# A graph attention layer on one core: two tiles of sources picked on the chip from the first step on, from parts of x made in the prologue

## The chip, the cores and the metric

The kernel runs on one core of a Trainium2 chip. The metric is the device time of one execution in microseconds (us): before the change the median of 10 runs is 3075.61 us (3069.55 to 3079.59). Lower is better.

A core has five engines with queues of their own: PE (TensorE, matmuls; the profile shows its weight loads apart as PEld), DVE (VectorE), ACT (ScalarE), POOL (GpSimd, which here issues the indirect DMAs) and SP (SyncE, which issues plain DMAs). Each works through its instructions in order and waits on semaphores for the others.

## The reference

One layer of attention over the edges of a graph with 6250 nodes and 206250 edges, 64 channels in 4 heads of 16, then a residual and a layer norm. The edges are sorted by destination.

```
Qh, Kh, Vh = x @ Wq.T + bq, x @ Wk.T + bk, x @ Wv.T + bv      # per node, 4 heads of 16
Ee = edge_attr @ We.T + be                                    # per edge
score = (Kh[src] * Qh[dst] * (1 / sqrt(16)) * Ee).sum(-1)
score = exp(clip(score, -5, 5))
msg = Vh[src] * score[..., None]
wV = segment_sum(msg, dst, num_segments=6250)
out = layernorm(x + wV)
```

## The kernel before

**Tiles, groups, steps.** A tile is 128 edges, one on each partition; there are 1612. Eight tiles are a group (202 groups), and a step is two groups, save for the last eight steps, which are one group each. So steps 0 to 96 have 16 tiles and steps 97 to 104 have 8 (the last one 4). `STEPS`, `NS` = 105, `groups_of`, `tiles_in` say this in the code.

**Prologue.** From the transposed x in SBUF (`xT_sb`, one column for each node) PE makes k and v of all nodes, which go to a table in HBM (`kv_tab`), and q in three bf16 parts, which go to another. POOL meanwhile gathers the rows of x for the sources of the first four groups (`XS`, L230). At the end of the prologue a loop over these four groups in halves of four tiles (from L370) turns them on PE (L375), copies the turned x to SBUF on ACT (L378, `xe`), multiplies it with the weights of k and v (L380, L382) and copies the result into the kv buffers (L384). So steps 0 and 1 need no gather. POOL gathers groups 4 to 7 (steps 2 and 3) from `kv_tab` (L402), one indirect DMA for a tile. Then a value is read that says whether a window of destinations is too wide; it isn't, and the main part follows.

**The main part** runs over the steps. For a step s, in short:

- `spread`, `onehot_rows`, `queries` (L555, L572, L577, L595): each edge's q comes from a window of rows of the q table (`fetch_queries`), by a matmul with a one-hot of its destination. They are made for step s+1 within step s.
- `edges` (L388, L391): the edge values.
- `products`, `scores`, `message` (L602, L603, L609 to L612, L619): DVE multiplies k, q and the edge values, reduces them to scores, and multiplies v with them. The multiplication with v, L619, is the last reader of the step's kv buffer. There are five such buffers (`KVB`), and `gather(s + 4)` on POOL waits for L619 of step s-1.
- `minus` (L622, L630, L632): the message is split in three bf16 parts. `sums` (L638): a matmul with a one-hot of destinations adds the message by destination, one step later; `add` (L652) adds it to the accumulator.
- `close`, `spreads`, `roots`, `norm`: finished blocks of 128 nodes are normalised and stored.

**Picks.** For the last two tiles of a step, k and v aren't gathered. Step s prepares this for step s+2, when `picks_in(s)` holds: s from 4 to `LAST` = 94. `sources` (ACT, L466) and `sources_turned` (PE, L471) spread the sources of the tile over the partitions; `hots` (DVE, L481) makes one-hots of all 50 blocks of nodes in two instructions for each tile; `picks` (PE, L491) multiplies them with the table `parts`: x of all nodes in three bf16 parts, 50 blocks of 128 nodes by 192 columns. That is 100 matmuls a step, in four quarters of 25. `picked`, `picked_turned` and `picked_kv` (L498, L505, L507, L513 to L516) add the three parts, turn the picked rows of x and make k and v of them. In the steps with picks 14 of 16 tiles are gathered. In every sixth step from 12 on one more tile is fetched by rows through SP (`fetch_rows`, L544), so that 13 are gathered.

**The table `parts`** lies in the pool `accp` of the main part and is filled in steps 0 to 3: a memset (L427), then for blocks of 8 (`TB`) a load of x by SP into `raw` (L448), two copies by ACT (L450, L451) and in `table_parts_rest` two subtractions by DVE (L456, L458) with a copy by ACT between them (L457).

The order in all queues is the program's order, written out by hand (the loop `for s in range(NS)` at the end of the main part); nothing is moved by a scheduler.

Of the kernel before, what the change touches and what calls it, by code (L numbers as in the profile page):

```python
# [37 lines left out]
CB = 10  # L38
KVB = 5
XG = 4  # L40
TB = 8
M0 = 4
PAD = N
SPARE = N + 1
TABLES = 4
# [15 lines left out]

LAST = NS - 8 - 3


def picks_in(s):
    return M0 <= s <= LAST

# [33 lines left out]
def tile_gnn(ctx: ExitStack, tc: tile.TileContext, x, xT, wT, bias, beT, weT, eT, src, dst, dst_rows,  # L103
# [50 lines left out]
    be_p = consts.tile([3, G, C], BF16, name="be_p")  # L154
    wkv = consts.tile([P, 2, 2 * C], F32, name="wkv")
    bkv_p = consts.tile([3, G // 2, 2 * C], BF16, name="bkv_p")
    minus_b = consts.tile([P, P], BF16, name="minus_b")

    acc = consts.tile([P, RING, 4, C], F32, name="acc")
# [24 lines left out]
    with tc.tile_pool(name="nodes", bufs=1) as nodes, \  # L184
# [182 lines left out]
            fetch_queries(g)  # L367


        for g in range(XG):  # L370
            for h in range(2):
                tp = npsum.tile([P, 2, P], F32, name="tp", bufs=2)
                for u in range(2):
                    j = 4 * h + 2 * u
                    nc.tensor.transpose(tp[:, u, :],  # L375
                                        XS[g][:, j:j + 2, :].rearrange("p j c -> p (j c)"), ident)
                xe = nodes.tile([P, 2, P], F32, name="xe", bufs=2)
                nc.scalar.activation(xe, tp, AF.Copy)  # L378
                pv = npsum.tile([P, 4, 2 * C], F32, name="pv", bufs=2)
                nc.tensor.matmul(pv, ones_b, bkv_p, start=True, stop=False, skip_group_check=True)  # L380
                for u in range(2):
                    nc.tensor.matmul(pv[:, 2 * u:2 * u + 2, :], xe[:, u, :], wkv, start=False,  # L382
                                     stop=u == 1, skip_group_check=True)
                nc.scalar.activation(kv_of(g)[:, 4 * h:4 * h + 4, :], pv, AF.Copy)  # L384

    def edge_values(pe, et, n):

# [6 lines left out]
    def keys(t0):  # L394

        n = min(KEYS, T - t0)
        nc.vector.tensor_scalar(key_i[:, :n], dst_i[:, t0:t0 + n], P - 1, None, op0=OP.bitwise_and)
        nc.vector.tensor_copy(key[:, t0:t0 + n], key_i[:, :n, None].to_broadcast([P, n, 2]))

    def gather_kv(g, j):  # L400
        t = g * G + j
        nc.gpsimd.indirect_dma_start(  # L402
            out=kv_of(g)[:, j, :], out_offset=None, in_=kv_tab[:, :],
            in_offset=bass.IndirectOffsetOnAxis(ap=src_i[:, t:t + 1], axis=0))

    for g in range(XG, 2 * KVB - 2):
        for j in range(G):
            gather_kv(g, j)

    rv = nc.values_load(n_wide[0:1, 0:1], min_val=0, max_val=NR2 * 4)  # L410

    with tc.If(rv == 0) as branch:

        with tc.tile_pool(name="work", bufs=2) as work, \
# [8 lines left out]
            pa = small[:, 4 * C:7 * C].rearrange("p (i c) -> p i c", i=3)  # L423
            nc.tensor.transpose(col, row_b[:, 0:1].to_broadcast([P, P]), ident_b)

            parts = accp.tile([P, NB, 3, C], BF16, name="parts")
            nc.vector.memset(parts, 0.0)  # L427
            NX = N // NB
            x_v = x.rearrange("(p b) c -> p b c", p=NX)
            n_picks = LAST - M0 + 1  # L430
            src_f = accp.tile([P, n_picks, 2], F32, name="src_f")
            t0 = (M0 + 3) * 2 * G - 2
            for i in range(2):
                nc.vector.tensor_copy(src_f[:, :, i],
                                      src_i[:, t0 + i:t0 + i + 2 * G * (n_picks - 1) + 1:2 * G])
            pick = fixed.tile([P, 4 * P], F32, name="pick")
            rows3 = pick[:, :6 * C].rearrange("p (k i c) -> p k i c", k=2, i=3)
            HOT, FAR, X = {}, {}, {}
# [2 lines left out]

                return ap.rearrange("p (a b) -> p a b", b=2)

            def table_parts(b):

                n = min(TB, NB - b)
                raw = work.tile([P, TB, C], F32, name="raw", bufs=1)
                nc.sync.dma_start(raw[:NX, :n], x_v[:, b:b + n, :])  # L448
                rest = pick[:NX, :n * C].rearrange("p (b c) -> p b c", b=n)
                nc.scalar.activation(rest, raw[:NX, :n], AF.Copy)  # L450
                nc.scalar.activation(parts[:NX, b:b + n, 0], raw[:NX, :n], AF.Copy)  # L451
                return rest

            def table_parts_rest(b, rest):
                n = min(TB, NB - b)
                nc.vector.tensor_sub(rest, rest, parts[:NX, b:b + n, 0])  # L456
                nc.scalar.activation(parts[:NX, b:b + n, 1], rest, AF.Copy)  # L457
                nc.vector.tensor_sub(parts[:NX, b:b + n, 2], rest, parts[:NX, b:b + n, 1])  # L458

            def sources(s, i):  # L460

                if picks_in(s):
                    FAR[s, i] = work.tile([P, P], BF16, name="far")
                    nc.scalar.activation(FAR[s, i], row50, AF.Identity,  # L466
                                         bias=src_f[:, s - M0, i:i + 1], scale=-1.0)
# [42 lines left out]
            def picked_kv(s):  # L510
                if picks_in(s):
                    xe, kv = X.pop(s)
                    nc.tensor.matmul(kv, ones_b, bkv_p[:, :2], start=True, stop=False,  # L513
                                     skip_group_check=True)
                    nc.tensor.matmul(kv, xe, wkv, start=False, stop=True, skip_group_check=True)
                    nc.scalar.activation(kvs[(s + 2) % KVB][:, 2 * G - 2:, :], kv, AF.Copy)  # L516

            def gather(s):
                for g in groups_of(s):
                    for j in range(tiles_of(g)):  # L520
                        if is_rowed(s) and (g - STEPS[s][0]) * G + j == COLUMN:
# [58 lines left out]
            def onehot_edges(s):  # L580

                n, t0 = tiles_in(s), STEPS[s][0] * G
                OH[s] = work.tile([P, 2 * G, P], BF16, name="of")
                shape = [P, n, P // 2, 2]
                nc.vector.tensor_tensor(OH[s].rearrange("p t (a c) -> p t a c", c=2)[:, :n],  # L585
                                        pairs(col)[:, None].to_broadcast(shape),
                                        key[:, t0:t0 + n, None, :].to_broadcast(shape),
                                        op=OP.is_equal)
# [109 lines left out]
                                               op0=OP.mult, op1=OP.add)  # L698

            closed, scaled, normed = 0, 0, 0  # L700
            keys(0)
            for k, g in enumerate(groups_of(0)):
                onehot_rows(g, spread(g))
# [1 line left out]
                edges(0, k)  # L705
            queries(0)
            onehot_edges(0)
            for s in range(NS):
                more = s + 1 < NS
                for g in groups_of(s):  # L710
# [58 lines left out]
                if more:  # L769
# [29 lines left out]
    with branch.Else():  # L799

        sums = [dram.tile([NR, C], F32, name=f"sums{i}") for i in range(TABLES)]
        with tc.tile_pool(name="gconsts", bufs=1) as gc, \
                tc.tile_pool(name="gloads", bufs=3) as loads, \
                tc.tile_pool(name="ggath", bufs=4) as gath, \
# [28 lines left out]
            def gather(g, j):  # L833
                if j == 0:
                    Q[g] = gath.tile([P, G, C], F32, name="gq")
                t = g * G + j
                if g >= 2 * KVB - 2:
# [125 lines left out]
```

## Time and profile before

| | |
|---|---|
| median of 10 runs | 3075.61 us (3069.55 to 3079.59) |
| the profiled execution | 3076.17 us |
| its span, first to last instruction | 3074.4 us |
| mean granted clock of PE | 0.783 |
| busy: PE, PEld | 1982.7 us (64%), 1556.1 us (51%) |
| busy: DVE, ACT, POOL | 1503.4 us (49%), 917.4 us (30%), 1337.2 us (43%) |
| indirect gathers of kv (L402) | 1383, 1305.1 us on POOL |
| matmuls of the picks (L491) | 9100, 1042.5 us on PE |
| one-hots for the picks (L481) | 364, 651.4 us on DVE |

No engine is busy all the time, so shares of busy time don't tell what bounds the kernel; it has to be read from the length of single steps and what they wait for. In the profile a line such as `L491 PE MATMUL pick<-parts,hot` names the line of the code, the engine, the operation, and the tile written and those read. In a timeline, a line starts with the start and the duration of a run of such instructions; behind it stand, in brackets, the idle time of the engine before it and what ended that. "Issue" means that the profile shows nothing that it waited for; "remote" that the event which ended it can't be matched with an instruction. Times of the timeline are us from the start of the span.

### The profile page before, as it was taken

What the parts mean: (1) busy time and instruction counts of PE and PEld (TensorE: products, weight loads), DVE (VectorE), ACT (ScalarE), POOL (GpSimd) and SP (SyncE); (2) the same over time, 40 slices, a digit from 0 to 9 for tenths busy, and PEclk for the clock granted to TensorE, in tenths of its full rate; (3) what the DMA queues carried; (4) which work ended last, traced back from release to release, by engine and by line L of the source; (5) the groups of instructions that cost most, each with busy time, mean ns of one, the idle gap of its engine ahead of it and who ended that gap; (6) DMA issues with size and microseconds to landing.
All of it is one profiled execution on the core that took longest, in us unless ns stands there. A gap on an engine that the chain in (4) does not pass through costs nothing. (4 is left out here: it accounts for less than half of the span.)

```text
span 3074.4 us, 44286 instructions
## 1 busy us (share of the span) xinstructions
PE 1982.7 (64%) x15751; PEld 1556.1 (51%) x15751; DVE 1503.4 (49%) x1695; ACT 917.4 (30%) x1328; POOL 1337.2 (43%) x1427
## 2 busy tenths in 40 slices
PE   5546666757666666757566666757576666667675
PEld 4324554545455554545454554545454555545553
DVE  3244545545454545545454545545454545455554
ACT  2242232323233223323232322323232332223234
POOL 5454435344443434344444435344444434353332
PEclk9967878878787877778787877778787878777885
DMA  5222212111111212121211212121212112121121
GB/s 150 66 78 59 55 44 59 51 49 52 46 48 51 56 43 56 53 57 45 54 52 46 55 44 57 43 57 44 59 47 55 47 52 56 43 57 43 51 56 32
DMA packets 109970, 166.71 MB, mean 54 GB/s; under 512 B 69196, under 2 KB 71452, under 8 KB 109626
## 3 DMA queue, kind: packets, MB, share of 16 engines
q0 software_dynamic: 45280, 91.78, 11.7%
q1 hardware_dynamic: 64074, 71.01, 8.2%
q8 instruction: 125, 2.05, 0.3%
q10 hardware_dynamic: 384, 1.00, 0.2%
q14 instruction: 107, 0.88, 0.1%
HBM read 156.33 MB, written 7.33 MB: 53 GB/s over the span
## 5 line engine op out<-in xcount | busy, mean ns | idle before, releaser
L402 POOL DMA_INDIRECT kv<-kv_tab,src_i x1383 | 1305.1, 944 | 1680.7 <-DVE pq L619 1243.0
L491 PE MATMUL pick<-parts,hot 128*128 128x192 bf16 x9100 | 1042.5, 275 | 251.7 <-issue 251.2
L491 PEld LDWEIGHTS <-hot 128*128 128x128 bf16 x9100 | 892.0, 110 | 378.4 <-issue 322.8
L481 DVE TENSOR_TENSOR hot<-small,block 128x3200 bf16<-128x3200 bf16 x364 | 651.4, 1818 | 286.8 <-remote 246.1
L595 PE MATMUL pq<-qw,to 126*128 126x64 bf16 x1612 | 166.2, 221 | 682.3 <-issue 613.6
L572 ACT ACTIVATE to<-pb,minus_row 126x1024 bf16<-126x1024 f32 x202 | 222.9, 1103 | 971.7 <-PE pb L555 922.5
L602 DVE TENSOR_TENSOR prod<-kv,pq 128x1024 f32<-128x1024 f32 (+2 forms) x105 | 123.7, 1178 | 784.4 <-PE pq L595 406.0
L595 PEld LDWEIGHTS <-to 126*128 126x128 bf16 x1612 | 109.2, 113 | 755.6 <-issue 752.3
L632 ACT ACTIVATE msg<-pq 128x1024 bf16<-128x1024 f32 (+2 forms) x210 | 207.6, 989 | 751.7 <-remote 512.7
L391 PE MATMUL pe<-we_sb,et 128*128 128x128 f32 x1612 | 246.4, 298 | 0.0
L391 PEld LDWEIGHTS pe<-we_sb,et 128*128 128x128 f32 x1612 | 206.6, 201 | 54.0 <-issue 47.6
L577 ACT ACTIVATE to<-to,one_p 126x1024 bf16<-126x1024 bf16 x202 | 230.4, 1141 | 3.5
L609 DVE TENSOR_REDUCE small<-prod 128x64 f32<-128x1024 f32 (+2 forms) x105 | 124.4, 1185 | 196.0 <-PE small L471 147.7
L638 PEld LDWEIGHTS <-of 128*128 128x128 bf16 x1612 | 156.7, 108 | 49.1 <-issue 39.2
L638 PE MATMUL small<-msg,of 128*128 128x192 bf16 x1612 | 171.5, 265 | 0.5 <-ACT msg L632 0.5
L630 PE MATMUL pq<-msg,minus_b 128*128 128x512 bf16 x404 | 128.1, 396 | 66.0 <-ACT msg L622 54.1
L555 PE MATMUL pb<-key_rows,ident_b 112*128 112x512 bf16 x403 | 152.6, 467 | 7.3 <-ACT to L572 4.1
L622 ACT ACTIVATE msg<-pq 128x1024 bf16<-128x1024 f32 (+2 forms) x105 | 103.8, 989 | 96.0 <-DVE pq L619 96.0
L603 DVE TENSOR_TENSOR prod<-prod,pe 128x1024 f32<-128x1024 f32 (+2 forms) x105 | 123.6, 1177 | 3.6
L619 DVE TENSOR_TENSOR pq<-kv,small 128x1024 f32<-128x1024 f32 (+2 forms) x105 | 123.5, 1176 | 1.3 <-ACT small L612 1.3
L585 DVE TENSOR_TENSOR of<-small,key 128x2048 bf16<-128x2048 bf16 (+2 forms) x105 | 123.2, 1174 | 0.3
L498 DVE TENSOR_REDUCE xp<-pick 128x128 f32<-128x384 f32 x91 | 50.7, 558 | 103.3 <-PE pick L491 103.3
(129 smaller groups left out, 991.4 us busy)
## 6 DMA issues: line engine op xcount, KB each, us to landing
et<-in_eT SPq DMA_DIRECT2D x100, 512.0 KB
rk<-kv_tab SPq DMA_DIRECT2D x1920, 0.5 KB
kv<-kv_tab,src_i POOLq DMA_INDIRECT x1383
qw<-q_tab SPq DMA_DIRECT2D x202, 15.8 KB
kv_tab<-kv_sb SPq DMA_DIRECT2D x5, 640.0 KB
q_tab<-q SPq DMA_DIRECT2D x5, 480.0 KB
acc<-in_x SPq DMA_DIRECT2D x48, 32.0 KB
out<-y SPq DMA_DIRECT2D x48, 32.0 KB
```

The source lines that it names most:

```text
L391: nc.tensor.matmul(pe[:, 2 * u:2 * u + 2, :], et[:, u, :], we_sb, start=False, stop=u == n // 2 - 1, skip_group_check=True)
L402: nc.gpsimd.indirect_dma_start(out=kv_of(g)[:, j, :], out_offset=None, in_=kv_tab[:, :], in_offset=bass.IndirectOffsetOnAxis(ap=src_i[:, t ...
L481: nc.vector.tensor_tensor(HOT[s, i, h].rearrange("p b (a c) -> p b a c", c=2), pairs(from_b[i])[:, None].to_broadcast(shape), block2[:, bl ...
L491: nc.tensor.matmul(rows3[:, i], hot[:, k, :], parts[:, b], start=b == 0, stop=b == NB - 1)
L555: nc.tensor.matmul(pb[:, b:b + 4, :], ident_b[:NR2, g // 2:g // 2 + 1].to_broadcast([NR2, P]), key_rows[:, g % 2, b * P:(b + 4) * P], star ...
L572: nc.scalar.activation(TO[g][:, :n, :], pb[:3 * W, :n, :], AF.Square, bias=minus_row3[:3 * W])
L577: nc.scalar.activation(TO[g][:, :n, :], TO[g][:, :n, :], AF.Relu, bias=one_p[:3 * W], scale=-1.0)
L595: nc.tensor.matmul(PQ[s][:, (g - STEPS[s][0]) * G + j, :], TO[g][:, j, :], QW[g], start=j == 0, stop=j == tiles_of(g) - 1, skip_group_chec ...
L609: nc.vector.tensor_reduce(score, prod[:, :n, :].rearrange("p g (h d) -> p g h d", h=H), axis=AX.X, op=OP.add)
L630: nc.tensor.matmul(msg[:, lo:hi, :], minus_b, M3[s][:, lo:hi, i, :], start=False, stop=True, skip_group_check=True)
L632: nc.scalar.activation(M3[s][:, :n, i + 1, :], msg[:, :n, :], AF.Copy)
L638: nc.tensor.matmul(PA[s], OH[s][:, j, :], M3[s][:, j], start=j == 0, stop=j == n - 1)
```

## The change

- The table `parts` moves from `accp` to the constants and is made in the prologue, within the loop over the first four groups. `x_turned` does the turning of a half, `first_kv` its matmuls and copy; the next half is turned before the present one is multiplied. Between them stand `parts_of_x` for two blocks of four (`TB` is now 4): PE turns columns of `xT_sb` into a PSUM tile (`ps`, four buffers), ACT copies the first part, DVE subtracts it; and behind `first_kv`, `rest_of_x` makes the second and third part. All 50 blocks are made so, in the first seven of eight halves.
- The memset, the loads of `raw` and the copies and subtractions in steps 0 to 3 go away, `table_parts` and `table_parts_rest` with them.
- Picks run from step 0 to `LAST` = 96, instead of 4 to 94. So the picked tiles are those of steps 2 to 98, of which 97 and 98 are of one group (`picked_kv` and `src_f` allow for 8 tiles). `sources`, `sources_turned` and `hots` for step 0 stand before the loop.
- `is_picked` says for a tile whether it is picked; the gathers of such tiles are left out, in the prologue (groups 5 and 7) too.
- The branch for too wide windows, which isn't taken, gathers what is missing and has one buffer less in `ggath`.

```diff
-TB = 8
-M0 = 4
+TB = 4
...
-LAST = NS - 8 - 3
+LAST = NS - 8 - 1
 
 def picks_in(s):
-    return M0 <= s <= LAST
+    return 0 <= s <= LAST
+
+def is_picked(g, j):
+    s = max(s for s in range(NS) if STEPS[s][0] <= g)
+    return picks_in(s - 2) and g == groups_of(s)[-1] and j >= G - 2
...
+    parts = consts.tile([P, NB, 3, C], BF16, name="parts")
...
-        for g in range(XG):
-            for h in range(2):
...
+        def x_turned(g, h):
+            tp = npsum.tile([P, 2, P], F32, name="tp", bufs=2)
+            for u in range(2):
+                j = 4 * h + 2 * u
+                nc.tensor.transpose(tp[:, u, :], XS[g][:, j:j + 2, :].rearrange("p j c -> p (j c)"),
+                                    ident)
+            xe = nodes.tile([P, 2, P], F32, name="xe", bufs=2)
+            nc.scalar.activation(xe, tp, AF.Copy)
+            return xe
+
+        def first_kv(g, h, xe):
+            pv = npsum.tile([P, 4, 2 * C], F32, name="pv", bufs=2)
+            nc.tensor.matmul(pv, ones_b, bkv_p, start=True, stop=False, skip_group_check=True)
+            for u in range(2):
+                nc.tensor.matmul(pv[:, 2 * u:2 * u + 2, :], xe[:, u, :], wkv, start=False,
+                                 stop=u == 1, skip_group_check=True)
+            nc.scalar.activation(kv_of(g)[:, 4 * h:4 * h + 4, :], pv, AF.Copy)
+
+        halves = []
+
+        def parts_of_x(b):
+            n = min(TB, NB - b)
+            px = npsum.tile([P, 2, 2 * C], F32, name="ps").rearrange("p i (j c) -> p (i j) c", j=2)
+            px = px[:, :n]
+            for u in range(n):
+                nc.tensor.transpose(px[:, u, :], xT_sb[:C, (b + u) * P:(b + u + 1) * P],
+                                    ident[:C, :C])
+            nc.scalar.activation(parts[:, b:b + n, 0], px, AF.Copy)
+            nc.vector.tensor_sub(px, px, parts[:, b:b + n, 0])
+            halves.append((px, b, n))
+
+        def rest_of_x():
+            px, b, n = halves.pop(0)
+            nc.scalar.activation(parts[:, b:b + n, 1], px, AF.Copy)
+            nc.vector.tensor_sub(parts[:, b:b + n, 2], px, parts[:, b:b + n, 1])
+
+        order = [(g, h) for g in range(XG) for h in range(2)]
+        blocks = list(range(0, NB, TB))
+        xe = x_turned(*order[0])
+        for i, gh in enumerate(order):
+            following = x_turned(*order[i + 1]) if i + 1 < len(order) else None
+            for b in blocks[2 * i:2 * i + 2]:
+                parts_of_x(b)
+            first_kv(*gh, xe)
+            xe = following
+            while halves:
+                rest_of_x()
...
     for g in range(XG, 2 * KVB - 2):
         for j in range(G):
-            gather_kv(g, j)
+            if not is_picked(g, j):
+                gather_kv(g, j)
...
-            parts = accp.tile([P, NB, 3, C], BF16, name="parts")
-            nc.vector.memset(parts, 0.0)
...
+            src_f = accp.tile([P, LAST + 1, 2], F32, name="src_f")
+            full = NS - 8 - 2
             for i in range(2):
...
+            for s in range(full, LAST + 1):
+                t0 = STEPS[s + 2][0] * G + G - 2
+                nc.vector.tensor_copy(src_f[:, s], src_i[:, t0:t0 + 2])
...
-                    nc.scalar.activation(kvs[(s + 2) % KVB][:, 2 * G - 2:, :], kv, AF.Copy)
+                    n = tiles_in(s + 2)
+                    nc.scalar.activation(kvs[(s + 2) % KVB][:, n - 2:n, :], kv, AF.Copy)
...
-                        if not picks_in(s - 2) or g == STEPS[s][0] or j < G - 2:
+                        if not is_picked(g, j):
                             gather_kv(g, j)
...
+            sources(0, 0)
+            sources_turned(0, 0)
             keys(0)
...
             onehot_edges(0)
+            sources(0, 1)
+            sources(1, 0)
+            for h in range(2):
+                hots(0, 0, h)
             for s in range(NS):
...
-                making = [b for b in range(s * 2 * TB, (s + 1) * 2 * TB, TB) if b < NB]
-                if making:
-                    rest = table_parts(making[0])
...
-                for i, b in enumerate(making):
-                    if i:
-                        rest = table_parts(b)
-                    table_parts_rest(b, rest)
```

More of the change, by code (lines that the diff above doesn't have):

```diff
@@ L367, in tile_gnn @@
             fetch_queries(g)
-        for g in range(XG):
-            for h in range(2):
[L372 to L384, printed above, removed]
+        def x_turned(g, h):
[7 more added lines that the diff above has]
+            return xe
@@ L424, in tile_gnn @@
             nc.tensor.transpose(col, row_b[:, 0:1].to_broadcast([P, P]), ident_b)
-            parts = accp.tile([P, NB, 3, C], BF16, name="parts")
-            nc.vector.memset(parts, 0.0)
[L428 to L432, printed above, removed]
-            for i in range(2):
-                nc.vector.tensor_copy(src_f[:, :, i],
-                                      src_i[:, t0 + i:t0 + i + 2 * G * (n_picks - 1) + 1:2 * G])
+            src_f = accp.tile([P, LAST + 1, 2], F32, name="src_f")
+            full = NS - 8 - 2
+            for i in range(2):
+                t0 = 3 * 2 * G - 2 + i
+                nc.vector.tensor_copy(src_f[:, :full, i],
+                                      src_i[:, t0:t0 + 2 * G * (full - 1) + 1:2 * G])
+            for s in range(full, LAST + 1):
+                t0 = STEPS[s + 2][0] * G + G - 2
+                nc.vector.tensor_copy(src_f[:, s], src_i[:, t0:t0 + 2])
             pick = fixed.tile([P, 4 * P], F32, name="pick")
@@ L442, in pairs @@
                 return ap.rearrange("p (a b) -> p a b", b=2)
[L444 to L458, printed above, removed]
             def sources(s, i):
@@ L466, in sources @@
                     nc.scalar.activation(FAR[s, i], row50, AF.Identity,
-                                         bias=src_f[:, s - M0, i:i + 1], scale=-1.0)
+                                         bias=src_f[:, s, i:i + 1], scale=-1.0)
             def sources_turned(s, i):
@@ L803, in tile_gnn @@
                 tc.tile_pool(name="gloads", bufs=3) as loads, \
-                tc.tile_pool(name="ggath", bufs=4) as gath, \
+                tc.tile_pool(name="ggath", bufs=3) as gath, \
                 tc.tile_pool(name="gwork", bufs=2) as work, \
@@ L836, in gather @@
                 t = g * G + j
-                if g >= 2 * KVB - 2:
+                if g >= 2 * KVB - 2 or is_picked(g, j):
                     gather_kv(g, j)
```

## The prediction

> **What bounds the kernel now.** I read the page first, for the costliest groups:
>
> ```profile
> L402 POOL DMA_INDIRECT kv<-kv_tab,src_i x1383 | 1305.1, 944 | 1680.7 <-DVE pq L619 1243.0
> L491 PE MATMUL pick<-parts,hot 128*128 128x192 bf16 x9100 | 1042.5, 275 | 251.7 <-issue 251.2
> ```
>
> POOL gathers for 1305 us of 3074 and idles 1243 us waiting for L619, the instruction of `message` that frees a kv buffer. So gathering isn't the rate of the kernel; POOL waits for the steps. The picks are the largest group of TensorE.
>
> Next I took the start of L619 of every step from the timeline and asked for the busy time of each engine between one start and the next ("interval s": from L619 of step s to that of step s+1). The columns are the stretch, its length, then busy time and count on PE, PEld, DVE, ACT, POOL, then granted clock, DMA share and GB/s. Intervals 0 to 4, 6 and 7:
>
> ```profile
> 153.46:178.54 25.08, 11.37 (x63) 7.07 (x63) 9.19 (x12) 11.09 (x15) 15.08 (x16) 0.64 0.31 84
> 178.54:203.12 24.58, 11.40 (x58) 7.43 (x58) 9.60 (x14) 11.19 (x15) 13.21 (x14) 0.64 0.30 81
> 203.12:226.60 23.48, 11.89 (x59) 7.87 (x59) 9.50 (x14) 10.47 (x16) 13.22 (x14) 0.57 0.29 78
> 226.60:250.16 23.56, 13.86 (x77) 9.37 (x76) 11.83 (x18) 8.55 (x12) 13.21 (x14) 0.64 0.25 65
> 250.16:279.62 29.46, 18.23 (x148) 14.27 (x148) 14.48 (x14) 8.07 (x11) 13.22 (x14) 0.75 0.19 52
> ...
> 310.41:341.07 30.66, 19.98 (x167) 15.79 (x165) 14.49 (x14) 8.65 (x13) 13.20 (x14) 0.78 0.19 49
> 341.07:368.66 27.59, 19.39 (x167) 15.08 (x165) 15.36 (x18) 8.64 (x13) 12.27 (x13) 0.81 0.21 54
> ```
>
> This table decides the case. Intervals 1 to 3 and 6 all gather 14 tiles. Without picks they take about 24 us, with a hundred picks 30.66. So a hundred picks cost some 6.5 us of the path. Two more gathers cost little: interval 0 has 16 and lasts 25.08. Interval 7 has 13 (a tile fetched by rows) and lasts 3 us less than interval 6.
>
> The same at the end, intervals 92 to 96, all with 8 gathers; picks stop within the third:
>
> ```profile
> 2897.52:2921.42 23.90, 19.00 (x167) 15.64 (x165) 15.40 (x18) 8.54 (x13) 7.54 (x8) 0.86 0.18 47
> 2921.42:2945.36 23.94, 19.25 (x167) 15.55 (x165) 14.48 (x15) 8.25 (x12) 7.55 (x8) 0.86 0.17 47
> 2945.36:2966.55 21.19, 17.85 (x154) 14.27 (x153) 11.84 (x16) 8.06 (x11) 7.54 (x8) 0.92 0.18 51
> 2966.55:2981.98 15.43, 9.48 (x58) 6.36 (x59) 6.91 (x10) 6.70 (x10) 7.54 (x8) 0.78 0.25 69
> 2981.98:2996.36 14.38, 7.31 (x39) 4.46 (x39) 5.65 (x12) 5.51 (x6) 7.55 (x8) 0.62 0.20 44
> ```
>
> The fetches by rows (L544) also begin at step 4 and end with step 93, so the first table alone could be their doing; here 21.19 to 15.43 has no fetch by rows on either side and shows 75 picks worth 5.76 us.
>
> Last, the timeline of a usual step says why picks aren't hidden, although PE idles in the early steps. Gathers run here from 1301.98 to 1319.1:
>
> ```profile
> 1303.47 2.23 PE L491 MATMUL pick<-parts,hot 128*128 128x192 bf16 x25
> ...
> 1315.52 0.21 PE L595 MATMUL pq<-qw,to 126*128 126x64 bf16 x1 [1.23 <-issue]
> ...
> 1318.30 0.21 PE L595 MATMUL pq<-qw,to 126*128 126x64 bf16 x1 [2.58 <-issue]
> ...
> 1322.23 4.19 PE L491 MATMUL pick<-parts,hot 128*128 128x192 bf16 x25
> ```
>
> Twenty-five picks go by in 2.23 us at first; some 5 us into the gathers PE thins out to single matmuls, until they end; then the last 25 picks (4.19 us) and the rest of the step follow in series. What stalls PE there the profile doesn't say ("issue"); it is the same in the early steps, where 9.01 us of DVE's idle before L609 at 175.87 are put to "remote". Idle PE time under gathers is thus not free room for picks.
>
> **The change part by part.** *Prologue.* A half of the k-and-v loop takes 3.03 us (L375 to L375):
>
> ```profile
> 124.12 0.63 PE L375 MATMUL tp<-ident,xs 128*128 128x128 f32 x2
> ...
> 125.29 1.35 PEld L382 LDWEIGHTS pv<-wkv,xe 128*128 128x128 f32 x4 [0.51 <-ACT xe L378]
> ...
> 127.16 0.63 PE L375 MATMUL tp<-ident,xs 128*128 128x128 f32 x2
> ```
>
> It ends with the last copy of ACT at 139.54, and the first matmul of the main part starts at 139.56: the loop is on the path. Turning the next half first removes the wait of 0.51 us for `xe` in each half. Added are 50 turns of x, eight in each of the first six halves and two in the seventh. The nearest row is L375: two turns in 0.63 us, 0.42 us for one, so one each 0.21 us. Six halves gain 8 x 0.213 - 0.51 = 1.19 us (7.1), the seventh 0.43 - 0.51, the last -0.51: **+6.5 us**. Bounds: half the columns at half the price, 0.107 each, +1.2; as the multiplication L350 (64 columns, two records of 0.22 us for each), +17. ACT gets four copies of 0.38 us (the row of L322, 128x256) a half, 2.5 of 4.2 us with its own; DVE gets 26 subtractions, 0.5 us each by L353 and L458, under its idle stretch of 21.01 us before L427. Both are covered by PE; without that cover DVE's 13 us would count. SP loses the seven loads of `raw`, behind which later edge and query loads queue in steps 0 to 3; no long wait for those shows, so nothing is gained.
>
> *Entry of step 0.* The first turn of sources now stands before the first `spread` on PE: two casts of 0.14 us and two small ones on DVE, 0.34 on ACT, 0.22 on PE and handing over, an estimate of **+1.3 us** (0 to 2). The two `hots` before `products(0)`, 2 x 1.82 us, fall where the memset L427 (4.06 us) goes away; without that, +3.6. On POOL four prologue gathers go (1.25 us apart) and two for step 4; POOL waited 16.27 us for the branch and 11.92 for L619 there, so **0**.
>
> *Steps 0 to 3 with picks.* Intervals 0 to 4 were 25.08 + 24.58 + 23.48 + 23.56 + 29.46 = 126.2. I price each by pick intervals already there with 14 gathers (29.46, 30.79, 30.66, 30.60: mean 30.4): 151.9, **+25.7 us**. In this the two gathers saved in interval 0 and the removed work on ACT and DVE (0.59 + 0.62 us before the exponential of a step) are contained. If all picks hid: 0.
>
> The clock is granted at 0.57 to 0.64 in intervals 0 to 3 and 0.78 in interval 6. The Trainium skill (TensorE: Matmul & The Clock Gate, "HAM oscillation — how this bites in real kernels") warns that a gap of about 3.4 us idle puts PE back to half rate, so added matmuls should pay for themselves in part. By that rule alone, as an estimate, 11.4 us of PE work at 0.64 would shrink by some 4 us in four intervals and the total would be 16 us lower. The row that bears on it is interval 4: its clock is 0.75 already, and it lasts 29.46, so I take nothing off.
>
> *Steps 95 and 96 with picks; two gathers fewer for 97 and 98.* Intervals 92 and 93 gather 6 tiles instead of 8: (30.66 - 23.90)/6 = 1.13 us for each gather, -4.5 in all (0 to -12, the latter by interval 7's 3.07). Interval 94 becomes like 93: +2.75. Interval 95 likewise: 23.94 - 15.43 = +8.5. Interval 96 gets 75 picks: +5.8. Interval 97 gets the reduction (0.56), turn, copy and kv matmul of the last pick behind which the next step's products wait: +1.5 (0 to 2). Sum **+14** (6 to 19).
>
> Sum: 6.5 + 1.3 + 25.7 + 14 = +47.5. The profiled execution took 3076.17 (span 3074.4 and 1.8 around it), 0.56 above the median of the runs: 3075.6 + 47.5 = **3123**.
>
> **The rivals.** *Dear turns* (12%): as L350, +17 in the prologue and all else as forecast, 3134. For it: the same 64 columns. Against: L375 is a turn itself.
>
> *Early picks hide* (13%): PE is busy for only 11.4 of 24.6 us in interval 1, and 100 picks at 2.23/25 = 0.089 us are 9. Then only prologue, entry and tail count: 3075.6 + 6.5 + 1.3 + 14 = 3097. Against: interval 4.
>
> *Gathers decide* (6%), the other side: each gather taken out of an interval is worth the 3.07 us between 30.66 (14) and 27.59 (13), and the picks lie in the PE idle time. Six gathers lie in intervals (step 5 in interval 0, steps 97 and 98 in 92 and 93): -18.4, + 7.8 for prologue and entry: 3065. It decides from the point where intervals 0 to 3 stay under 24 us with picks. For it: interval 7. Against: 8 gathers and 14 differ by 1.13 each, and interval 0 with 16 lasts 25.08.
>
> *Nothing but the prologue* (5%): picks hide at both ends and gathers are worth nothing; 3083 at most, less if the turns are cheap (3078). That all steps are rebuilt is certain from the code: 9700 picks and 1371 gathers.
>
> **How the numbers follow.** Forecast 64%. The bounds of its own terms give 3075.6 + 1.2 + 0 + 22 + 6 = 3105 to 3075.6 + 17 + 2 + 28 + 19 = 3142 (early steps at 29.6 to 30.8). With the second rival the range is **3092 to 3142**. What a measurement of this kernel can tell from no change is about 0.2%, 6 us. Faster 6%, same 5%, slower 89%.
>
> **What would show it.** In the changed profile: turns in the prologue's halves 4.2 us apart; first `message` near 161 us instead of 153.46; intervals 0 to 3 near 30 us, with clock 0.75 to 0.8; intervals 95 and 96 near 24 and 20; intervals 5 to 91 as before. I'm wrong if intervals 0 to 3 stay near 24, or if the usual step itself changes: the new places of tiles in memory touch all 87 of these, 0.3 us each would be 26 us, and nothing in the trace lets me predict that.

## The result, and the profile after

| | before | after |
|---|---|---|
| median | 3076.33 us (3069.55 to 3081.22, 30 runs) | 3102.72 us (3095.3 to 3108.15, 9 runs) |
| the profiled execution: span, granted clock | 3074.4 us, 0.783 | 3104.3 us, 0.792 |

The changed kernel is slower: the ratio is 1.0083, with a 95% interval of 1.0074 to 1.0093. Forecast were 3123 us, with a range of 3092 to 3142. The medians differ by 26.4 us, the two profiled executions by 30 (3106.26 against 3076.17).

The page of the changed kernel, its costliest groups (busy us, mean ns of one, then idle time before them and what ended most of it):

```profile
L440 POOL DMA_INDIRECT kv<-kv_tab,src_i x1371 | 1293.7, 944 | 1721.7 <-DVE pq L642 1278.5
L513 PE MATMUL pick<-parts,hot 128*128 128x192 bf16 x9700 | 1110.2, 274 | 268.5 <-issue 267.3
```

All the code was meant to do is there: 12 gathers fewer, 600 picks more. POOL still waits for the steps, now 1278.5 us for L642 (`message`, L619 before).

The windows from one `message` to the next, of the changed kernel, intervals 0 to 5 and 91 to 97 (stretch, length, then busy time and count on PE, PEld, DVE, ACT, POOL, then granted clock, DMA share, GB/s):

```profile
156.41:187.03 30.62, 20.65 (x175) 17.28 (x175) 14.16 (x12) 8.41 (x11) 13.20 (x14) 0.83 0.12 31
187.03:216.64 29.61, 20.41 (x171) 15.64 (x169) 14.40 (x14) 8.98 (x13) 13.21 (x14) 0.77 0.20 51
216.64:246.15 29.51, 20.27 (x164) 15.51 (x162) 14.38 (x14) 8.83 (x13) 13.22 (x14) 0.77 0.19 51
246.15:275.45 29.30, 19.19 (x170) 15.53 (x168) 15.37 (x18) 8.63 (x13) 13.21 (x14) 0.83 0.20 52
275.45:305.89 30.44, 19.27 (x167) 15.64 (x165) 14.49 (x14) 8.64 (x13) 13.21 (x14) 0.78 0.19 50
305.89:336.50 30.61, 19.44 (x167) 15.57 (x165) 15.47 (x19) 8.64 (x13) 13.22 (x14) 0.78 0.20 51
2895.80:2923.38 27.58, 19.75 (x168) 15.29 (x167) 14.32 (x15) 8.64 (x13) 12.27 (x13) 0.81 0.20 52
2923.38:2941.90 18.52, 16.29 (x167) 13.40 (x165) 15.21 (x17) 8.53 (x13) 5.66 (x6) 1.00 0.20 53
2941.90:2962.05 20.15, 17.76 (x167) 14.77 (x165) 14.48 (x15) 8.53 (x13) 5.66 (x6) 0.92 0.19 49
2962.05:2984.30 22.25, 18.82 (x164) 15.74 (x162) 15.29 (x18) 8.65 (x13) 7.55 (x8) 0.85 0.18 49
2984.30:3005.59 21.29, 18.16 (x170) 15.44 (x168) 14.48 (x14) 6.94 (x11) 7.54 (x8) 0.92 0.19 51
3005.59:3024.30 18.71, 15.02 (x131) 11.76 (x129) 9.57 (x15) 5.96 (x8) 7.55 (x8) 0.91 0.11 29
3024.30:3032.74 8.44, 6.15 (x31) 3.83 (x31) 4.21 (x9) 4.79 (x8) 5.66 (x6) 0.74 0.39 105
```

Intervals 0 to 3 last what a usual step lasts. In the intervals with a hundred picks and few gathers the length goes with the granted clock: with 6 gathers 18.5 us at 1.00 and 20.2 at 0.92, with 8 gathers 21.3 at 0.92 and 22.3 at 0.85; that comes back below.

Cut at the same places, the two profiles account for all of the 29.9 us between their spans:

| stretch | before | after | difference | forecast |
|---|---|---|---|---|
| start to the first `message` | 153.46 | 156.41 | +3.0 | +7.8 |
| intervals 0 to 4 | 126.16 | 149.48 | +23.3 | +25.7 |
| intervals 5 to 91 | 2617.90 | 2617.49 | -0.4 | 0 |
| intervals 92 to 103 | 165.37 | 169.45 | +4.1 | +14 |

### The profile page after: what moved, and what is told of

It is laid out like the page before. It is cut to its first block, busy times and chain, and to the rows that moved or that the text cites. A ratio compares the mean times of both kernels' runs of the same rounds, so it can differ in the third digit from the quotient of the medians.

```text
span 3104.3 us, 45728 instructions
## 1 busy us (share of the span) xinstructions
PE 2045.7 (66%) x16437; PEld 1609.1 (52%) x16437; DVE 1545.4 (50%) x1738; ACT 922.0 (30%) x1357; POOL 1325.7 (43%) x1415
## 5 line engine op out<-in xcount | busy, mean ns | idle before, releaser
L440 POOL DMA_INDIRECT kv<-kv_tab,src_i x1371 | 1293.7, 944 | 1721.7 <-DVE pq L642 1278.5
L513 PE MATMUL pick<-parts,hot 128*128 128x192 bf16 x9700 | 1110.2, 274 | 268.5 <-issue 267.3
L513 PEld LDWEIGHTS <-hot 128*128 128x128 bf16 x9700 | 944.3, 109 | 406.2 <-issue 347.1
L503 DVE TENSOR_TENSOR hot<-small,block 128x3200 bf16<-128x3200 bf16 x388 | 694.1, 1818 | 279.2 <-remote 245.3
L595 ACT ACTIVATE to<-pb,minus_row 126x1024 bf16<-126x1024 f32 x202 | 223.0, 1104 | 1011.0 <-PE pb L578 1003.5
L661 PE MATMUL small<-msg,of 128*128 128x192 bf16 x1612 | 169.3, 263 | 0.5 <-ACT msg L655 0.5
L653 PE MATMUL pq<-msg,minus_b 128*128 128x512 bf16 x404 | 123.9, 385 | 21.3 <-ACT msg L645 12.7
L642 DVE TENSOR_TENSOR pq<-kv,small 128x1024 f32<-128x1024 f32 (+2 forms) x105 | 123.5, 1177 | 0.3 <-ACT small L635 0.3
```

The costliest lines, as they stand in the source:

```text
L440: nc.gpsimd.indirect_dma_start(out=kv_of(g)[:, j, :], out_offset=None, in_=kv_tab[:, :], in_offset=bass.IndirectOffsetOnAxis(ap=src_i[:, t ...
L503: nc.vector.tensor_tensor(HOT[s, i, h].rearrange("p b (a c) -> p b a c", c=2), pairs(from_b[i])[:, None].to_broadcast(shape), block2[:, bl ...
L513: nc.tensor.matmul(rows3[:, i], hot[:, k, :], parts[:, b], start=b == 0, stop=b == NB - 1)
L595: nc.scalar.activation(TO[g][:, :n, :], pb[:3 * W, :n, :], AF.Square, bias=minus_row3[:3 * W])
L653: nc.tensor.matmul(msg[:, lo:hi, :], minus_b, M3[s][:, lo:hi, i, :], start=False, stop=True, skip_group_check=True)
L661: nc.tensor.matmul(PA[s], OH[s][:, j, :], M3[s][:, j], start=j == 0, stop=j == n - 1)
```

## The experiments

The runs came to three chips, and that matters more here than any edit. On one (called H below, as in the expectations) the kernel before takes 3075.58 us, on the two others (F) 1790.2 and 1790.0 to 1790.6 us. The chip of the result above isn't on record; its times are those of H. What separates H from F in the traces is the stretch of a step in which PE starts only single matmuls while POOL gathers; it is called the hold-up below. Each run is compared only with the kernel before on its own chip. e5 to e7 ran on H, e1 to e4 and e8 to e12 on F. The expectations of e1 to e4 were written when only H was known.

**e5_change: the changed kernel itself, on H.**

> The changed kernel as it is, beside the runs of the kernel before on the same chip. Two kinds of chip have to be told apart: the one of the prediction, where the kernel before takes 3076 us and TensorE is held up while gathers run (H), and the one of the first four experiments, where the kernel before takes 1790 us and the trace shows no such hold-up (F). Theory (picks are worth it only where they lie beside gathers; under the hold-up they are serial): on H a ratio of 1.008 to 1.009 again; on F steps 0 to 3 cost no more than they do without picks (17 us with 14 gathers at 1.25 each is their floor, 20 without the picks), so the ratio is 0.990 to 1.000. Rival (picks are serial TensorE work everywhere): 1.01 on F as well, from 4 x 6 us in steps 0 to 3 and 14 us at the end.

Measured 3107.5 us against 3075.58, ratio 1.0099 (1.0085 to 1.0114): the loss again, as the theory had it for H, if slightly above its figure.

**e6_start and e7_end: the two halves of the change, on H.** Each has the parts in the prologue.

```diff
# e6_start
-    return 0 <= s <= LAST
+    return 0 <= s <= LAST - 2
# e7_end
-    return 0 <= s <= LAST
+    return 4 <= s <= LAST
```

> The changed kernel with picks in steps 0 to 94 only: the prologue's parts and the early picks, without the two added steps at the end. Theory on H: 3099 us, the prologue's +3 and the early steps' +23 without the end's +4; the ratio 1.007 to 1.009. On F: 0.985 to 1.000, not slower than the kernel with the prologue's parts alone (0.9999). Rival (early picks serial on F too): 1.010 to 1.015.

> The changed kernel with picks in steps 4 to 96: the prologue's parts and the two added steps at the end, without the early picks. Theory on H: 3083 us, ratio 1.002 to 1.003, of which the end has +4 and the prologue up to +3. On F: 0.998 to 1.004; these steps have 6 to 8 gathers (7.5 to 10 us), which don't bind there, so picks in them cost up to 2 x 4 us and save two gathers each in steps where nothing waits for them.

Measured: e6_start 3097.86 us, 1.0061 (1.0047 to 1.0075); e7_end 3086.14 us, 1.0029 (1.0017 to 1.0041). The early picks give most of the loss, somewhat below the ratio that was expected; the end alone gives a small one, as expected. Taken from e5_change, the end is worth 0.38% (some 12 us) and the early picks 0.70% (21 us), and nothing that can be told from zero is left for the prologue; these differences have the errors of two ratios, about 0.2% each. For the end the profiles give only 4 us: intervals 5 to 91, whose program is the same in both, took 2621.7 us in e5_change and 2612.0 in e6_start, so most of the 12 us is scatter.

The windows of e7_end, intervals 0 to 4 without and 92 to 96 with added picks:

```profile
159.45:184.86 25.41, 12.62 (x73) 8.78 (x73) 6.59 (x8) 7.97 (x9) 15.13 (x16) 0.79 0.16 45
184.86:208.90 24.04, 9.35 (x58) 5.78 (x58) 6.91 (x9) 8.05 (x9) 13.23 (x14) 0.64 0.24 73
208.90:231.85 22.95, 9.34 (x59) 5.81 (x59) 6.91 (x10) 7.91 (x10) 13.25 (x14) 0.72 0.17 50
231.85:255.35 23.50, 12.40 (x77) 8.19 (x76) 11.34 (x15) 8.29 (x11) 13.23 (x14) 0.65 0.23 65
255.35:285.06 29.71, 18.85 (x149) 15.28 (x149) 14.48 (x15) 8.09 (x11) 13.24 (x14) 0.70 0.18 51
...
2902.33:2920.80 18.47, 16.28 (x167) 13.41 (x165) 15.21 (x17) 8.53 (x13) 5.67 (x6) 1.00 0.19 54
2920.80:2940.93 20.13, 17.74 (x167) 14.84 (x165) 14.48 (x14) 8.53 (x13) 5.69 (x6) 0.92 0.17 48
2940.93:2963.03 22.10, 18.96 (x164) 15.52 (x162) 15.30 (x18) 8.78 (x13) 7.56 (x8) 0.85 0.17 49
2963.03:2984.39 21.36, 18.11 (x170) 15.46 (x168) 14.39 (x15) 6.93 (x11) 7.56 (x8) 0.92 0.18 52
2984.39:3003.03 18.64, 14.70 (x131) 11.87 (x129) 9.57 (x16) 5.96 (x8) 7.56 (x8) 0.91 0.10 29
```

With the early picks taken out, intervals 0 to 4 fall back to 125.6 us (126.2 before the change), although `parts` is no longer made in them. So the 23 us are the picks' and their one-hots', and removing the old work on `parts` from these steps gave next to nothing (0.5 us). The tail is that of the full change to 0.2 us in each interval, and costs 169.3 - 165.4 = 3.9 us; in e6_start it is 164.4. The rest of e7_end's excess is in its first `message` at 159.45.

**e1_prologue and e10_prologue_again: the parts in the prologue alone**, picks in steps 4 to 94.

```diff
-    return 0 <= s <= LAST
+    return 4 <= s <= LAST - 2
```

> The changed kernel with picks from step 4 to 94 only, as before; the parts of x stay in the prologue. Theory (the prologue lies on the path, the table work in steps 0 to 3 was nearly hidden): first message 3 us late as in the profile after (156.4 against 153.5), intervals 0 to 3 near 24 us, so 3077 to 3082. Rival (taking the table work out of steps 0 to 3 pays for the prologue: 1.2 us of copies before each exponential, twelve DMAs and copies fewer): 3068 to 3075.

> The prologue's parts alone (picks in steps 4 to 94 as before). On H: the loop over k and v is longer by 8 halves of 1 us, but its start moves with the stage before it, which the hold-up makes irregular: first message 2 to 6 us later than 153.46, intervals unchanged, ratio 1.000 to 1.003; that the prediction's 6.5 us count in full would give 1.002 to 1.004. If the loop is hidden: 0.999 to 1.0005. On F: 0.9999 again.

Both ran on F: 1789.81 and 1789.93 us, ratio 0.9999 (0.999 to 1.0008) each time. What this version takes on H was not measured; the expectation for H stays open. On F its cost is hidden, and the page of e10_prologue_again says by what (the chain of waits by engine, then the group of gathers):

```profile
POOL 29%; PE 27%; DVE 21%; issue 13%; DMA 8%; ACT 2%; DVEq 0%; SPq 0%; POOLq 0%; ACTq 0%
...
L440 POOL DMA_INDIRECT kv<-kv_tab,src_i x1383 | 1305.4, 944 | 421.6 <-issue 384.4
```

On F POOL waits for nothing but its own issue once it has begun: 1383 gathers of 0.944 + 0.30 us follow one another, from 43 us to 1769 us. A later first `message` (83.83 in e1_prologue, 94.96 in e10_prologue_again, both with a span of 1788.2) doesn't matter, because POOL isn't held by it.

**e11_change_again: the changed kernel on F.**

> The changed kernel as it is, meant for a chip where the kernel before takes 1790 us (F); on H a ratio of 1.008 to 1.010 again. On F, theory (picks are worth it where they lie beside gathers): intervals 0 to 3 go from the 14 to 14.5 us that gathers already made leave them to 15 to 17, the tail saves little, ratio 0.997 to 1.004. Rival (early picks serial on F as well): intervals 0 to 3 longer by 6 us each, ratio 1.010 to 1.015.

Measured 1782.81 us against 1790.56, ratio 0.9953 (0.9939 to 0.9967): the change makes the kernel *faster* there, a little beyond what was expected. Its first five windows:

```profile
95.36:110.27 14.91, 14.91 (x165) 13.14 (x164) 13.89 (x13) 8.42 (x11) 10.43 (x12) 1.00 0.19 49
110.27:126.23 15.96, 15.96 (x171) 13.76 (x169) 14.29 (x14) 8.86 (x13) 12.00 (x14) 1.00 0.31 90
126.23:141.88 15.65, 15.65 (x167) 13.44 (x165) 14.21 (x15) 8.55 (x13) 11.69 (x14) 1.00 0.30 87
141.88:157.83 15.95, 15.95 (x171) 13.75 (x169) 15.18 (x18) 8.63 (x13) 12.19 (x13) 1.00 0.31 91
157.83:173.26 15.43, 15.43 (x163) 13.12 (x161) 14.21 (x15) 8.53 (x13) 11.57 (x13) 1.00 0.31 89
```

Against e10_prologue_again they sum to 77.9 instead of 66.7 us (+11.2; PE is busy all the time in them, so the picks cost PE time here too), but intervals 5 to 91 go from 1472.0 to 1453.3 us (-18.6). POOL's lead accounts for both. It gathers from 43 us on, held only once by a `message` (the first, for 1.4 us), and at first the steps lag behind it. Later they follow it: from step 25 on in e10_prologue_again, and from step 38 on in e11_change_again, `message` comes some 7 to 9 us behind the start of the last gather of its step. So the longer early steps only use up POOL's lead, and when step 92 is reached the number of gathers decides: 8 of the 12 that go lie before it, 8 x 1.25 = 10 us, and it is reached 7.0 us sooner (1626.6 instead of 1633.6). The last four save nothing more, since steps 97 on no longer follow POOL. Intervals 0 to 3 are 14.9 to 16.0 us long, where 15 to 17 was expected.

And a stretch of a usual step of e11_change_again, the timeline of PE; gathers follow one another all the while:

```profile
763.85 2.23 PE L513 MATMUL pick<-parts,hot 128*128 128x192 bf16 x25
...
767.18 2.23 PE L513 MATMUL pick<-parts,hot 128*128 128x192 bf16 x25
769.24 0.63 PE L618 MATMUL pq<-qw,to 126*128 126x64 bf16 x16
769.71 2.23 PE L513 MATMUL pick<-parts,hot 128*128 128x192 bf16 x25
```

It is the same program as on H, where these 16 matmuls (L595 before the change) come one at a time over several us and the 25 picks after them take 4 us. On F there is no hold-up.

**e2_none, e8_none_again, e12_none_third: no picks**, all tiles gathered.

```diff
-    return 0 <= s <= LAST
+    return False
```

> The changed kernel without any pick: all 16 tiles of each step are gathered (13 to 14 before), the 9700 matmuls and 388 one-hots are gone. Theory (a hundred picks cost 6 us of serial PE time in a step and two gathers at most 2.5): intervals like interval 0 of before, 25 us, so some 5 us less in 95 steps, 2580 to 2680. Rival (each gather beyond thirteen costs the 3.07 us between intervals of 14 and 13): intervals of 30 us and more, 3050 to 3400.

> No picks at all, all tiles gathered, 16 a step, meant for a chip where the kernel before takes 3076 us (H; where it takes 1790, F, 2017 us and a ratio of 1.127 again). Theory (under the hold-up an interval is the gathers' run and the rest of the step in series, and 100 picks are 5 to 6 us of that rest): intervals near 25 us as interval 0 of the kernel before had with 16 gathers and no picks; 92 of them at 5 us less than 30.1 give 2610 us, 2520 to 2720, so on H the picks were never worth it. Rival 1 (every gather costs the 3 us between 14 and 13): 16 gathers without picks take 30 us, 3050 us. Rival 2 (the hold-up needs the picks' own work): the gathers' pace alone binds as on F, 20 us, 2150 us.

> No picks at all, 16 gathers a step. On F 2017 us again. On H, theory (the gathers' run and the rest of the step in series; 100 picks are 5 to 6 us of that rest): intervals near 25 us, 2610 us, 2520 to 2720. Rival 1 (each gather costs the 3 us between 14 and 13): 30 us, 3050 us. Rival 2 (the hold-up needs the picks' own work): 20 us, 2150 us.

All three ran on F: 2017.15, 2016.98 and 2017.27 us, ratios 1.1268, 1.1267 and 1.1266. From e12_none_third, the timeline of DVE and the group of gathers on the page:

```profile
856.48 1.22 DVE L625 TENSOR_TENSOR prod<-kv,pq 128x1024 f32<-128x1024 f32 x1 [11.40 <-DMA kv<-kv_tab,src_i]
```

```profile
L440 POOL DMA_INDIRECT kv<-kv_tab,src_i x1565 | 1477.8, 944 | 477.1 <-issue 460.3
```

Nearly every step waits for its gathers, 11.40 us in this one, and a usual interval is 20.0 us, 16 x 1.25. From 1383 to 1565 gathers the span grows from 1788.2 to 2015.3, 1.25 us for each: over this range the kernel on F is the number of gathers times POOL's pace, and picks pay. From 1383 to 1371 it falls by only 7.5 us, as said above. What the kernel without picks takes on H, which would have told the price of all its picks there at once, was never measured.

**e3_paced: POOL slowed**, an iota of 0.25 us behind each gather.

```diff
+            pad = accp.tile([P, P], I32, name="pad")
...
                         if not is_picked(g, j):
                             gather_kv(g, j)
+                            nc.gpsimd.iota(pad, pattern=[[1, P]], base=0, channel_multiplier=0)
```

> The changed kernel with a small operation on POOL (an iota of 128x128, 0.22 us in the prologue) behind each gather of the main part, so that gathers start some 1.5 us apart instead of 1.25. Theory (PE is held up for as long as the run of gathers lasts): the run of 14 gets 3 to 4 us longer and each interval with it, 3350 to 3450. Rival (PE is held up only when gathers come faster than something drains them; at 1.42 us in the prologue PE's events were not late): intervals fall to 24 to 27 us, 2550 to 2850.

On F 1951.18 us, ratio 1.09 (1.088 to 1.092), a mean interval of 18.5 against 16.7 us in e11_change_again. It was meant for the hold-up, which F doesn't have, and tells nothing about it; it only confirms that POOL's pace is felt there.

**e4_fewer and e9_fewer_again: half the gathers** of steps 5 to 96; the tiles left out keep old values.

```diff
-                        if not is_picked(g, j):
+                        if not is_picked(g, j) and (s < 5 or s > 96 or j % 2 == 0):
                             gather_kv(g, j)
```

> The changed kernel with every second gather of steps 5 to 96 left out (7 of 14; the tiles of the others keep what an earlier step left, so the output is not the reference's); picks and everything else as they are. Theory (the interval is the run of gathers plus the serial rest): between the intervals with 8 and with 6 gathers, 19 to 24 us, so 2250 to 2550. Rival (PE's own work bounds a step with picks, and the run of gathers only moves it about): 27 us and more, above 2800.

> The changed kernel with 7 of the 14 gathers of a step in steps 5 to 96 (the other tiles of kv are stale, so the output is not the reference's), picks kept. On H: theory (the hold-up lasts as long as the gathers): intervals near 20 us with a granted clock over 0.9, as the intervals with 6 gathers at the end of the changed kernel (18.5 and 20.1), total 2290 us, 2200 to 2400. Rival (the hold-up does not hang on the gathers but on the step's own work): intervals stay over 27 us, total over 2850. On F: 1684 us, ratio 0.941 again.

On F: 1683.8 and 1688.68 us, ratios 0.9406 and 0.9434. The busy line of e9_fewer_again's page:

```profile
PE 1636.0 (97%) x16437; PEld 1391.0 (83%) x16437; DVE 1521.7 (90%) x1738; ACT 914.3 (54%) x1357; POOL 732.9 (44%) x786
```

With the gathers halved PE is the bound, at intervals of 15.7 us. So on F the changed kernel, at 16.7 us, stands 1 us a step above what PE alone allows, and more picks would soon cost more than the gathers they save.

## Why the prediction was right

**The total alone doesn't show it.** 3102.7 us lies 20 us below the forecast, a little below the 3105 at which the bounds of its own terms end, and nearer to the 3097 of *early picks hide*. It is within the range only because the range was widened for that rival, which turned out wrong; this much is luck. What tells the forecast from its rivals is the length of single stretches.

**Early steps: right in mechanism and nearly in size.** The forecast was that a hundred picks cost some 6 us of the path on this chip because they lie in series with the hold-up. Intervals 0 to 3 came at 29.3 to 30.6 us; the sum was +23.3 instead of +25.7. e7_end takes the picks out again and the sum goes back to 125.6, so that they cost this much is shown. The rival *early picks hide* falls on H, and so does *gathers decide*: both need intervals 0 to 3 to stay near 24 us. That it is the hold-up which puts them in series is read from the timeline, not tried: no run on H takes the hold-up away. On F, where there is none, the same picks cost 11.2 us in intervals 0 to 4, so a part of the 23.3 may be plain PE time.

The granted clock did rise from 0.57 to 0.64 up to 0.77 to 0.83, as expected, and the sum came 2.4 us below the forecast, which had taken nothing off for it. The rule of the Trainium skill (TensorE: Matmul & The Clock Gate, "HAM oscillation — how this bites in real kernels"), that PE must have no idle gaps of more than about 3.4 us, had been turned into an estimate of 16 us paid back by the busier PE. The intervals speak against this estimate.

**The usual steps: right.** Intervals 5 to 91 moved by -0.4 us in all. That it is so little is chance, since in e5_change, e6_start and e7_end they take 2612.0 to 2621.7 us; but the 26 us that tiles at new places in memory might have cost would have shown, and didn't.

**The prologue: the loop right, its start not foreseen.** The first turn of the loop, in PE's timeline before the change:

```profile
114.95 0.69 PE L375 MATMUL tp<-ident,xs 128*128 128x128 f32 x2
```

The first turns and the second half in the changed kernel:

```profile
110.33 1.12 PE L380 MATMUL tp<-ident,xs 128*128 128x128 f32 x4
...
114.82 0.63 PE L380 MATMUL tp<-ident,xs 128*128 128x128 f32 x2
115.39 1.11 PE L401 MATMUL ps<-ident,xT_sb 64*128 64x64 f32 x8
116.43 0.60 PE L388 MATMUL pv<-bkv_p,ones_b 3*128 3x512 bf16 x1
116.97 2.08 PE L390 MATMUL pv<-wkv,xe 128*128 128x256 f32 x4
118.83 0.64 PE L380 MATMUL tp<-ident,xs 128*128 128x128 f32 x2
```

Eight turns take 1.11 us, 0.14 each instead of 0.213, and a half 4.01 us instead of 4.2. *Dear turns* falls. The loop, from its first turn to its last copy, grew from 25.2 to 32.6 us, +7.4 where 6.5 was forecast (32.8, 34.1 and 31.9 in e5_change, e6_start and e7_end). The prediction had ACT and DVE wholly covered by PE, but in the seventh half PE waits 1.2 us before its turns, 2.7 in e6_start (there for DVE's L410), none in e7_end. From the first turn to the first `message` the change adds 7.6 us, and 7.8 and 9.1 in e5_change and e6_start, where 7.8 was forecast. But the loop began at 110.33 instead of 114.95. The stage of q before it, in which PE waits up to 8.7 us at a time while POOL gathers, ends at another time in each execution: 109.5, 110.3 and 115.3 in e5_change, e6_start and e7_end, with the same program up to there. So the first `message` came at 155.8 to 159.5 in the four profiles on H, 2.3 to 6.0 us later than before. The forecast compared one execution's start with itself; the start has a scatter of some 5 us that one profile doesn't show. The entry of step 0 was priced at +1.3 and, from the loop's last copy to the first `message`, was +0.2 (13.3 to 13.5); in e7_end, without early picks, it is 12.3. So its own work does cost 1.2, and the memset that goes away gives 1.0 back, which the forecast had counted only as cover for the one-hots.

**The end: the term that was mis-sized**, +4.1 instead of +14. The step of the prediction was "(30.66 - 23.90)/6 = 1.13 us for each gather, -4.5 in all", and that added steps would be like 92 and 93. Measured: intervals 92 and 93 fell by 5.4 and 3.8 us, 9.2 for four gathers, 2.3 for each; and 94, 95 and 96 came 1.7, 2.6 and 1.5 us below the forecast. The first of these, 5.4, is read in PE's timeline. Before, interval 92 with 8 gathers:

```profile
2911.47 1.01 PE L595 MATMUL pq<-qw,to 126*128 126x64 bf16 x16 [2.25 <-ACT msg L632]
2912.29 4.19 PE L491 MATMUL pick<-parts,hot 128*128 128x192 bf16 x25
2916.27 1.00 PE L555 MATMUL pb<-key_rows,ident_b 112*128 112x512 bf16 x2
```

The same place after, with 6 gathers:

```profile
2933.39 0.59 PE L513 MATMUL pick<-parts,hot 128*128 128x192 bf16 x5 [0.47 <-issue]
2934.64 0.63 PE L618 MATMUL pq<-qw,to 126*128 126x64 bf16 x16 [0.66 <-ACT msg L655]
2935.10 2.23 PE L513 MATMUL pick<-parts,hot 128*128 128x192 bf16 x25
2937.16 0.60 PE L578 MATMUL pb<-key_rows,ident_b 112*128 112x512 bf16 x2
```

Counted from `message`, the 16 matmuls after the hold-up start at 11.26 instead of 13.95 us, 2.7 sooner, where two gathers less are 2 x 1.25. And what follows runs at full rate, 0.63 instead of 1.01, 2.23 instead of 4.19, 0.60 instead of 1.00 us; the granted clock of the interval is 1.00 instead of 0.86. That is 2.69 + 0.38 + 1.96 + 0.40 = 5.4 us, all of it. In interval 93 the hold-up ends equally soon, 11.26 us behind `message`, but the 25 picks still took 3.52 us, with a clock of 0.92, and the gain was 3.8. In e5_change, the same kernel, it is interval 93 that has the clock of 1.00: 92 and 93 last 20.1 and 18.5 us, the same 38.6 together. So with 6 gathers the clock falls in one of the two intervals and not in the other. The price of a gather under the hold-up is therefore a slope of about its pace plus a step of up to 2.7 us where the clock falls; the mean of 1.13, taken between 14 and 8 gathers, lies wholly on one side of that step. The forecast's bound of -12 for the four gathers, by 3.07 us for each, covers the 9.2. For 94 and 95 the row chosen was wrong: 92 and 93 contain fetches by rows and these two don't, and 8 gathers with a hundred picks then last 22.25 and 21.29 instead of 23.9. That the fetches are the cause is argued from this, not tried.

The two terms that came out smaller, by 4.8 at the front and 10 at the end, with 2.4 in the early steps and 0.4 in the usual ones, make up the 17.6 us between the forecast of 47.5 and the 29.9 of the profiles. *Nothing but the prologue* falls as well.

**What stays open.** Why PE is held up on H isn't settled. What can be shown is that it goes with the gathers: in the profile after, PE's starts thin out from 7.7 to 8.7 us behind `message` (6 to 7 us behind the first gather, where the prediction read 5) until 2.6 to 3.5 us behind the start of the last gather, at 11.3 us for 6 gathers, 12.8 for 8 and 21.4 for 14 (intervals 93, 94 and 41). In between, starts come some 0.7 us apart or at multiples of it (0.71, 1.41 and 2.11 us in interval 41). Pace and duration of a gather are the same on F (0.944 us), and so are its packets: by the share of their queue on the pages they take a mean of 127 ns in the kernel before (H) and in e1_prologue (F), 113 ns in e6_start (H) and e11_change_again (F). So slower gathers aren't it. The kernels that were to tell the cause apart, with fewer or slower gathers in all steps, came to run on F alone. Nor is it shown that the chip itself makes the difference: what else may have differed when each chip ran isn't on record.

## What to carry to other kernels

Moving work from a queue to an engine that looks idle pays only where the queue binds, and that is read from an interval with and without the work, not from busy shares: the same change is +0.8% where the steps bind (H) and -0.5% on a chip where the queue's pace does (F). When pricing the removal of one wait, look also at the clock behind it: where a shorter hold-up kept the clock up, it was worth 5.4 us instead of the 2.7 by which it was shorter. And a stage that is bound by irregular stalls should be given the scatter of several profiles, not the length in one.

## What was not expected of the hardware

The kernel before takes 3076 us on H and 1790 us on two other chips, 3069.6 to 3083.6 and 1789.5 to 1790.8 us over all its runs. Durations at full rate agree (a gather 944 ns, 25 picks 2.23 us); what differs is the hold-up of PE beside gathers and the granted clock (0.78 for the kernel before on H, 0.94 to 0.95 on F).

On F the loop over k and v ran at two speeds under one granted clock. The timeline of PE in e1_prologue:

```profile
60.05 0.63 PE L380 MATMUL tp<-ident,xs 128*128 128x128 f32 x2
60.62 1.11 PE L401 MATMUL ps<-ident,xT_sb 64*128 64x64 f32 x8
61.66 0.42 PE L388 MATMUL pv<-bkv_p,ones_b 3*128 3x512 bf16 x1
62.02 1.13 PE L390 MATMUL pv<-wkv,xe 128*128 128x256 f32 x4
62.98 0.38 PE L380 MATMUL tp<-ident,xs 128*128 128x128 f32 x2
63.30 0.70 PE L401 MATMUL ps<-ident,xT_sb 64*128 64x64 f32 x8
```

Within a half the same matmuls go from 2.08 to 1.13 us, and a half from 4.01 to 2.23; the granted clock is 1.00 in the windows on both sides. In e10_prologue_again and e11_change_again, and in all profiles on H, the loop stayed at the slow speed to its end. The Trainium skill (TensorE: Matmul & The Clock Gate, "Seeing it yourself") warns not to trust the records of the clock gate fully, event by event. This row fits that, though it doesn't show that the clock is the cause. On F the loop takes 20.4 us in e8_none_again and 31.3 in e11_change_again, by something that the granted clock of the profile doesn't show.
